# Pairs 0 and 1 of layer 0: residuals one pair later, pair 1's roots through TensorE, the second gate product ahead of the transposes

## The chip, the core and the metric

The kernel runs on one core of one Trainium2 chip. A core has TensorE (PE, matrix products into PSUM), VectorE (DVE), ScalarE (ACT), GpSimd (POOL), and SyncE (SP), whose queue issues the DMAs. Each engine works through its own queue in the order in which the program wrote it, and waits on semaphores for the others. The metric is the device time of one execution in microseconds; the median of three runs is compared.

## The reference

Two residual layers on one image `x` of 128 rows, 256 positions and 256 channels. Each layer first normalizes over 32 channel groups.

```
x = x + L0(_gn(x));   x = x + L1(_gn(x))        # _gn: 32 groups
L0:  m_norm = layer_norm(m);  z_norm = layer_norm(z)
     q, k, v = m_norm @ Wq.T, @ Wk.T, @ Wv.T    # 8 heads of 32
     b = z_norm @ Wb.T                          # bias per pair of positions and head
     gate = sigmoid(m @ Wg.T + bg)
     p = softmax(q k / sqrt(32) + b)            # 256 x 256 per row and head
     return (p v * gate) @ Wo.T + bo
L1:  4 heads of 64, softmax in a band of 16, projections w_in, w_out
```

Note that the gate is computed from `m` (the group-normalized rows), while Q, K and V are computed from `m_norm` (the same rows, layer-normalized over channels). Here `m` is `_gn(x)`, and the layer's result is added to `x`.

## The kernel before

**Stages.** A prologue loads `z` and `x`, takes the group statistics of `x` (tiles `M0` and `R0`, mean and reciprocal deviation per channel) and turns `z` into `eb`, the exponential of the bias for all heads. Layer 0 then walks over 64 pairs of rows; layer 1 follows. The change lies in the first three pairs of layer 0.

**One pair.** `class Pair` (L1244) holds the tiles of two rows of `x`. Its methods are steps:

- `centre` and `scale` (POOL) subtract `M0` and multiply by `R0`, giving `xg`. Each is one pass over 128x1024 values. `xg` has one buffer.
- `moments` (VectorE) takes the layer norm's statistics of `xg`, and `root` (POOL) raises the variances to the power -1/2, in place in one of two tiles `lrs`.
- `xgT`, the transposed group-normalized rows, is made in two ways. Pair 1 uses `turn`: eight TensorE transposes into two PSUM slots, and two ScalarE copies. From pair 2 on `blocks` loads 32x32 blocks of `x` by DMA, `turn_blocks` transposes them on VectorE and `scale_blocks` applies the group norm on ScalarE.
- `xnT`, the layer-normalized rows, is `xgT` times the roots, which must be spread over all partitions. `send` transposes the roots on VectorE and writes them to device memory with four DMAs; `fetch` reads them back into all partitions (`rs_r`); `normal` multiplies on POOL, in two halves. Pair 0, in the prologue, does it otherwise: `spread_roots` multiplies the roots, broadcast as weights, with the identity matrix on TensorE, and `normal_first` multiplies `xgT` by that PSUM tile on VectorE.
- `project` makes Q, K (from `xnT`) or the gate (from `xgT`), one half of the channels at a time: four matmul passes and one ScalarE eviction. `values` and `keep_values` make V.
- `scores(r, c)` makes the scores of row `r` and four heads and their exponentials; `add_bias` multiplies by `eb` on VectorE (`e`) and adds two key halves on POOL (`eboth`); `apply` makes the weighted values (`ov`) from `e` and the softmax sums (`su`) from `eboth` on TensorE; `gate` multiplies `ov` with the gate on VectorE.
- `invert` takes the reciprocals of the sums, and they go through device memory (`fetch_sums`); `normalize` applies them on POOL; `out_row` is the output product and `keep_row` adds `xt`.
- `residual` adds the output bias `bo` to `xt` on POOL, one pass over 128x1024 values. It must be done before the pair's first `keep_row`, and after `centre` has read `xt`.

**Order.** The loop over pairs, under `manual_schedule`, writes the order of every queue by hand. In turn `p`, `now` is pair `p`, `nxt` pair `p+1`, `nn` pair `p+2`, `was` pair `p-1` and `old` pair `p-2`; a name without a pair does nothing. The second half of a row's work is finished one pair later: `was.apply(1, es)` and `was.gate(1)` come in the next turn, `was.out_row(0)` at that turn's end and `old.out_row(1)` in the turn after. Turn 0 has a special order, since pair 1 isn't prepared in the same way as the later ones: `moments`, `root`, `send`, `fetch`, `turn`, `normal` for pair 1, and the residuals of pairs 1 and 0, stand inside it. The residual of a later pair stands at the end of the turn two before its own.

**Buffers.** Small products share two PSUM slots in turn (`mm`); a product waits until the slot's tile of two products ago has been read. Scores have two PSUM tiles, `eboth` two buffers for each half, `ov` and `su` one each.

Of the kernel before, what the change touches and what calls it, by code (L numbers as in the profile page):

```python
# [773 lines left out]
def fast_kernel(  # L774
# [215 lines left out]
    def mm(name):  # L990
        return ps_mm.tile([P, 512], F32, name=name, tag="mm")
# [544 lines left out]
    def some(n):  # L1536
        for _ in range(min(n, len(later))):
            later.pop(0)()
# [10 lines left out]
    def pair(p):  # L1549
        return Pair(p) if p < NP else Nobody()  # L1550
# [3 lines left out]
    def load_first():  # L1554

        by_block = x1[0][0:2].rearrange("s (i b) (k j a) -> k j b (s i) a", b=D0, k=KC, a=D0)
        for k in range(KC):
            for j in range(HQ):
                nc.sync.dma_start(
                    first[k][j * D0 : (j + 1) * D0].rearrange("b (i a) -> b i a", a=D0), by_block[k, j]  # L1560
                )
# [3 lines left out]
    now = nxt = nn = None  # L1565
# [131 lines left out]
    with tc.manual_schedule():  # L1697
        old = was = Nobody()
        es = nn3 = None
        for p in range(NP):  # L1700

            if p > 0:
                nxt.send()
            pss = now.scores(0, 0)
            if p == 0:
                now.values(0)
                now.keep_values(0)
                now.values(1)
            e0 = now.add_bias(0, 0, pss)
            was.apply(1, es)  # L1710
            if p == 0:
                now.keep_values(1)
                for r in range(2):
                    nxt.moments(r)
                nxt.root()
                nxt.send()
                now.project("gT", 0)
            pss = now.scores(0, 1)
            was.gate(1)
            nxt.fetch()  # L1720
            if p == 0:
                nxt.turn([mm("ps_x") for _ in range(KC)])
            es = e0, now.add_bias(0, 1, pss)
            if p == 0:
                nxt.normal()
            nn.centre()
            if p > 0:
                now.project("gT", 0)
                now.values(0)
                now.keep_values(0)  # L1730
            was.invert()
            was.fetch_sums()
            some(1 if p < NP - 2 else 3)
            nn.scale()
            now.project("gT", 1)
            if p > 0:
                nxt.turn_blocks()
            nn.blocks()
            if p == 0:
                nxt.residual()  # L1740
                now.residual()
            else:
                nxt.scale_blocks()
            if p < NP - 1:
                old.out_row(1)
                some(1 if p < NP - 2 else 3)
                old.keep_row(1)
                if p > 0:
                    now.values(1)
                    now.keep_values(1)  # L1750
            nn3 = pair(p + 3)
            if p > 0:
                nxt.normal()

            e0 = now.add_bias(1, 0, now.scores(1, 0))
            now.apply(0, es)
            pss = now.scores(1, 1)
            now.gate(0)
            es = e0, now.add_bias(1, 1, pss)
            was.normalize(0)  # L1760
            nn.moments(0)
            for m in range(KC):
                nxt.project("qT", m)
                nxt.project("kT", m)
            if p == NP - 1:
                load_first()
                old.out_row(1)
                old.keep_row(1)
                now.values(1)
                now.keep_values(1)  # L1770
                some(8)
            was.normalize(1)
            nn.moments(1)
            nn.root()
            nn.residual()
            some(3 if p < NP - 2 else 9)
            was.out_row(0)
            was.keep_row(0)
            old, was, now, nxt, nn = was, now, nxt, nn, nn3
        was.apply(1, es)  # L1780
        was.gate(1)
        was.invert()
        old.out_row(1)
        was.spread()
        old.keep_row(1)
        for r in range(2):
            was.normalize_last(r)
        for r in range(2):
            was.out_row(r)
            was.keep_row(r)  # L1790
        some(len(later))
# [29 lines left out]
    with tc.tile_pool(name="l1", bufs=2) as sb, tc.tile_pool(  # L1821
# [284 lines left out]
        def pair1(p):  # L2106
            return Pair1(p) if p < NP else Nobody()
# [36 lines left out]
        with tc.manual_schedule():  # L2144
            now, nxt = pair1(0), pair1(1)
# [18 lines left out]
            was = Nobody()  # L2164
            for p in range(NP - 1):
# [76 lines left out]
                was, now, nxt = now, nxt, nn  # L2242
# [44 lines left out]
@with_exitstack  # L2287
def mixer_kernel(ctx, tc, *args):

    nc = tc.nc  # L2290
    keep = ctx.enter_context(tc.tile_pool(name="verdict", bufs=1))
    verdict = keep.tile([1, 1], mybir.dt.int32, name="verdict")
    fast_kernel(tc, *args, verdict)
    again = nc.values_load(verdict[0:1, 0:1], min_val=0, max_val=1)
    with tc.If(again > 0):
        general_kernel(tc, *args)
# [53 lines left out]
```

## Time and profile before

| | |
|---|---|
| median of 3 runs | 3133.21 us (3131.51 to 3134.19) |
| the profiled execution's own time | 3134.36 us |
| its span, first to last instruction | 3132.6 us |
| mean granted TensorE clock | 0.985 |
| start of pair 0's first scores on TensorE | 215.93 us |
| start of pair 1's first scores | 242.27 us |
| start of pair 2's first scores | 277.68 us |
| start of pair 3's first scores | 305.11 us |

The profile is of one execution. The page gives each engine's busy time, its share in 40 slices of the span, the chain of work that ended last, and the costliest groups of instructions. The trace behind it can be cut to a stretch: the timeline lists an engine's instructions with the idle time before each and who ended it, and a table of stages gives the busy time of TensorE, its weight loads, VectorE, ScalarE and POOL, then the clock that TensorE was granted, the DMA engines' share and GB/s. The ends of matmuls are modelled: a group of matmuls that waits can be recorded as one long group without idle time. Instructions of one engine that follow each other overlap by a few hundredths of a microsecond in the records.

### The profile page before, as it was taken

How to read it: one execution, taken by the hardware profiler on the slowest of the kernel's cores; microseconds unless marked ns; L12 is line 12 of the kernel's file. 1: busy time of each engine (PE TensorE's matmuls, PEld its weight loads, DVE VectorE, ACT ScalarE, POOL GpSimd, SP SyncE). 2: the span in 40 equal slices, each digit the busy share in tenths (PEclk: the TensorE clock that was granted, in tenths of full speed). 3: DMA queues.
4: the chain of work that ended last, by engine and by line, in shares of the span. 5: the costliest groups of instructions: out<-in, count | busy, mean ns of one | idle time of the engine just before them, and what ended most of it. 6: DMA issues, size and time to landing. Idle time of an engine off the chain costs nothing.

```text
span 3132.6 us, 80584 instructions
## 1 busy us (share of the span) xinstructions
PE 3017.0 (96%) x33630; PEld 2096.3 (67%) x33630; DVE 2398.1 (77%) x4007; ACT 1574.6 (50%) x2639; POOL 2271.3 (73%) x1635
## 2 busy tenths in 40 slices
PE   5589999999999999999999999899999999999998
PEld 3345555655555565555555655588888888888886
DVE  7986777777777777777777777588888877777788
ACT  3454444444444444444444444355555555555554
POOL 3469998988899889889998987455555555555553
PEclk9799999999999999999999999899999999999999
DMA  9952333323333332333333232544343444343431
GB/s 360 389 173 59 97 71 99 93 66 91 99 99 69 99 97 65 89 98 99 69 99 99 64 92 71 117 93 94 92 95 92 95 92 94 90 97 88 98 93 53
DMA packets 690951, 328.16 MB, mean 105 GB/s; under 512 B 538673, under 2 KB 639921, under 8 KB 689425
## 3 DMA queue, kind: packets, MB, share of 16 engines
q1 hardware_dynamic: 686176, 320.28, 39.9%
q8 instruction: 266, 4.36, 0.6%
q10 hardware_dynamic: 4400, 2.63, 0.3%
q14 instruction: 109, 0.88, 0.1%
HBM read 254.09 MB, written 68.75 MB: 103 GB/s over the span
## 4 chain that ended last, share of the span: by engine, by line
PE 90%; DMA 4%; DVE 3%; issue 1%; POOL 1%; ACT 1%; SPq 0%; POOLq 0%; ACTq 0%; DVEq 0%
PE ps_p L1364 22%; PE ps_qk L1956 12%; PE ps_sc L1401 9%; PE ps_ov L1436 7%; PE ps_su_y L2088 7%; PE ps_v L1382 7%; PE ps_qk L1952 7%; PE ps_y L1491 7%; PE ps_o L2034 4%; PE ps_su L1444 3%; PE ps_sc L2009 3%; PE ps_su_y L2042 2%; DMA xa<-in_x_dram 1%; DVE st L1199 1%; DMA zt<-in_z_dram 1%
## 5 line engine op out<-in xcount | busy, mean ns | idle before, releaser
L1425 POOL TENSOR_TENSOR eboth<-e 128x512 f32<-128x512 f32 x512 | 746.9, 1479 | 175.9 <-PE ps_su L1444 95.5
L1421 DVE TENSOR_TENSOR e<-ps_sc,eb 128x1024 f32<-128x1024 f32 x384 | 458.2, 1221 | 290.5 <-ACT ps_sc L1413 289.9
L1413 ACT ACTIVATE ps_sc<-ps_sc 128x1024 f32<-128x1024 f32 x384 | 375.4, 1007 | 439.4 <-PE ps_sc L1401 308.0
L1401 PE MATMUL ps_sc<-qT,kT 32*128 32x256 f32 x4096 | 296.1, 401 | 0.1
L1919 POOL TENSOR_TENSOR dT<-xgT,dT 128x256 f32<-128x256 f32 x63 | 46.1, 731 | 315.7 <-ACT xgT L1905 315.7
L2020 POOL TENSOR_TENSOR e<-e,bw 128x384 f32<-128x384 f32 x256 | 248.4, 1001 | 10.7 <-ACT e L2018 10.7
L1401 PEld LDWEIGHTS ps_sc<-qT,kT 32*128 32x128 f32 x4096 | 186.3, 184 | 103.6 <-issue 90.6
L2088 PE MATMUL ps_su_y<-w_out,oT 128*128 128x256 f32 x1008 | 254.5, 385 | 0.9 <-DVE sums L2059 0.9
L1491 PEld LDWEIGHTS ps_y<-wo,oT 128*128 128x128 f32 x1024 | 194.7, 190 | 83.9 <-issue 44.7
L1364 PE MATMUL ps_p<-xgT,wg 128*128 128x512 f32 x512 | 249.1, 609 | 1.6 <-ACT xgT L1333 1.6
L1364 PE MATMUL ps_p<-xnT,wq 128*128 128x512 f32 x512 | 247.5, 605 | 1.5 <-POOL xnT L1351 1.4
L1436 PE MATMUL ps_ov<-e,v 128*32 128x256 f32 x4096 | 248.2, 383 | 0.0
L1491 PE MATMUL ps_y<-wo,oT 128*128 128x256 f32 x1024 | 243.1, 381 | 3.5 <-POOL oT L1481 2.7
L1382 PE MATMUL ps_v<-wv,xnT 128*128 128x256 f32 x1024 | 242.2, 379 | 0.0
L1364 PE MATMUL ps_p<-xnT,wk 128*128 128x512 f32 x512 | 240.7, 592 | 0.0
L1382 PEld LDWEIGHTS ps_v<-wv,xnT 128*128 128x128 f32 x1024 | 194.9, 190 | 54.7 <-issue 31.5
L2065 DVE RECIPROCAL rv<-sums 128x256 f32<-128x256 f32 x128 | 223.1, 1743 | 0.0
L1965 ACT ACTIVATE u<-ps_qk,bin_c 128x256 f32<-128x256 f32 x378 | 174.7, 477 | 94.9 <-PE ps_qk L1956 94.9
L2088 PEld LDWEIGHTS ps_su_y<-w_out,oT 128*128 128x128 f32 x1008 | 181.8, 190 | 22.4 <-DVE sums L2059 1.3
L1436 PEld LDWEIGHTS ps_ov<-e,v 128*32 128x32 f32 x4096 | 120.2, 110 | 109.2 <-issue 42.5
L1364 PEld LDWEIGHTS ps_p<-xnT,wk 128*128 128x128 f32 x512 | 97.2, 190 | 122.8 <-issue 122.8
L1371 ACT ACTIVATE gT<-ps_p,bg_c 128x512 f32<-128x512 f32 x128 | 88.0, 687 | 179.5 <-PE ps_p L1364 179.5
(229 smaller groups left out, 6553.3 us busy)
## 6 DMA issues: line engine op xcount, KB each, us to landing
xa<-in_x_dram SPq DMA_DIRECT2D x8, 4096.0 KB
xt<-in_x_dram SPq DMA_DIRECT2D x64, 512.0 KB
x<-xo SPq DMA_DIRECT2D x16, 2048.0 KB
xt<-x SPq DMA_DIRECT2D x64, 512.0 KB
rvb<-rsum SPq DMA_DIRECT2D x252, 128.0 KB
xs<-x SPq DMA_DIRECT2D x252, 128.0 KB
out_dram<-yo SPq DMA_DIRECT2D x63, 512.0 KB
xs<-in_x_dram SPq DMA_DIRECT2D x248, 128.0 KB
```

The costliest lines, as they stand in the source:

```text
L1364: nc.tensor.matmul(ps, w[:, k, m * P : (m + 1) * P], getattr(self, src)[:, k, :], start=(k == 0), stop=(k == KC - 1),)
L1382: nc.tensor.matmul(self.ps_v[:, b * C : (b + 1) * C], self.xnT[:, k, t * P : (t + 1) * P], wv[:, k, :], start=(k == 0), stop=(k == KC - 1),)
L1401: nc.tensor.matmul(self.pss[q // 2][:, q % 2, b, :], self.kT[rs, c, r * I + b * P : r * I + (b + 1) * P], self.qT[rs, c, r * I : (r + 1) * I],
L1413: nc.scalar.activation(self.pss[a], ps, AF.Exp)
L1421: nc.vector.tensor_tensor(es[a], pss[a], eb[:, h : h + 2], ALU.mult)
L1425: nc.gpsimd.tensor_tensor(t, es[a][:, :, 0, :], es[a][:, :, 1, :], ALU.add)
L1436: nc.tensor.matmul(ov[q * D0 : (q + 1) * D0, c, :], self.v[:, r, b, h * D0 : (h + 1) * D0], es[q // 2][:, q % 2, b, :], start=(b == 0), st ...
L1491: nc.tensor.matmul(self.ps_y[:, b * C : (b + 1) * C], self.oT[r][:, k, b * P : (b + 1) * P], wo[:, k, :], start=(k == 0), stop=(k == KC - 1),)
L1956: nc.tensor.matmul(to, lhs, rhs, start=start, stop=True, skip_group_check=True)
L2020: nc.gpsimd.tensor_tensor(e[:, q], e[:, q], bcast(bw.rearrange("p b w -> p (b w)"), 1, KC), ALU.mult)
L2065: nc.vector.reciprocal(self.rv[:, r, :], self.sums)
L2088: nc.tensor.matmul(self.y[:, b], self.oT[r][:, k, b * P : (b + 1) * P], w_out[:, k, :], start=(k == 0), stop=(k == KC - 1),)
```

## The change

Four things are moved or replaced, all in turns 0 to 2.

1. Roots of pair 1. `send`, `fetch` and `normal` of turn 0 go. In their place `spread_roots` stands after the products of `scores(1, 0)`, and `normal_first` after `add_bias(1, 0)`. This takes a VectorE transpose, five DMAs and two POOL passes out of turn 0, and puts in four TensorE products and two VectorE passes.
2. The second gate product of pair 0, `project("gT", 1)`, moves from after `nn.scale` to before `add_bias(0, 1)` and the transposes of pair 1. In TensorE's queue it now stands between the products of `scores(0, 1)` and the transposes, in ScalarE's its eviction stands before the two copies.
3. `add_bias(0, 1)` is written before `turn`. The order on each queue is not altered by this alone.
4. The residuals of pairs 1 and 0 leave turn 0. Pair 0's now stands in turn 1 and pair 1's in turn 2, after `nxt.normal` and before the `eboth` of `scores(1, 0)` in POOL's queue.

In SP's queue the loads of pair 2's blocks and of pair 3's rows now follow directly on the prologue's last loads. From turn 3 on all queues are as before.

```diff
                 for r in range(2):
                     nxt.moments(r)
                 nxt.root()
-                nxt.send()
                 now.project("gT", 0)
             pss = now.scores(0, 1)
             was.gate(1)
-            nxt.fetch()
+            if p > 0:
+                nxt.fetch()
+            else:
+                now.project("gT", 1)
+            es = e0, now.add_bias(0, 1, pss)
             if p == 0:
                 nxt.turn([mm("ps_x") for _ in range(KC)])
-            es = e0, now.add_bias(0, 1, pss)
-            if p == 0:
-                nxt.normal()
             nn.centre()
...
             nn.scale()
-            now.project("gT", 1)
             if p > 0:
+                now.project("gT", 1)
                 nxt.turn_blocks()
             nn.blocks()
-            if p == 0:
-                nxt.residual()
-                now.residual()
-            else:
+            if p > 0:
                 nxt.scale_blocks()
...
             if p > 0:
                 nxt.normal()
-
-            e0 = now.add_bias(1, 0, now.scores(1, 0))
+            if p in (1, 2):
+                was.residual()
+
+            pss = now.scores(1, 0)
+            if p == 0:
+                nxt.spread_roots()
+            e0 = now.add_bias(1, 0, pss)
+            if p == 0:
+                nxt.normal_first()
             now.apply(0, es)
```

## The prediction

> **What bounds the kernel now.** I read the page first: busy shares and slices, then the chain that ended last.
>
> ```profile
> PE 3017.0 (96%) x33630; PEld 2096.3 (67%) x33630; DVE 2398.1 (77%) x4007; ACT 1574.6 (50%) x2639; POOL 2271.3 (73%) x1635
> ...
> PE   5589999999999999999999999899999999999998
> ...
> PE 90%; DMA 4%; DVE 3%; issue 1%; POOL 1%; ACT 1%; SPq 0%; POOLq 0%; ACTq 0%; DVEq 0%
> ```
>
> TensorE is 90% of the chain. A microsecond that TensorE gains early in layer 0 is kept only if it is full from there on. So the second view is the chain cut to 150 to 420 us, around the pairs that the change touches.
>
> ```profile
> 240.71 4.69 POOL xt L1289 x2
> 245.40 4.88 POOL eboth L1425 x4
> 250.28 0.99 POOL lrs L1306
> 251.51 1.12 DVE e L1421
> 252.67 2.08 PE ps_sc L1401 x12
> 254.75 3.71 PE ps_p L1364 x4
> ```
>
> Here POOL, not TensorE, sets the end from 240.7 to 251.3: two residual adds, then pair 0's four `eboth` sums, then the roots of pair 2, whose transpose stands first in VectorE's queue. After 252.67 every long piece of this chain is PE. The third view is TensorE's timeline of the same place, with its idle time and who ended it.
>
> ```profile
> 226.10 1.98 PE L1364 MATMUL ps_p<-xgT,wg 128*128 128x512 f32 x4 [1.55 <-ACT xgT L1333]
> ...
> 234.83 2.36 PE L1364 MATMUL ps_p<-xnT,wq 128*128 128x512 f32 x4 [1.35 <-POOL xnT L1351]
> ...
> 246.67 0.63 PE L1444 MATMUL ps_su<-eboth,pick 128*32 128x256 f32 x4 [1.39 <-POOL eboth L1425]
> ```
>
> Three stalls: the second gate product waits for the copies of pair 1's transposes, Q of pair 1 waits for `xnT` behind the roots' trip through memory, and the sums of pair 0 wait for POOL. The fourth view, busy time by stages of 3.41 us, shows what the last one drags behind it: the clock column (after ACT and POOL) falls.
>
> ```profile
> 245.31:248.72 3.41, 1.25 (x8) 0.29 (x8) 0.00 (x0) 0.08 (x1) 3.41 (x4) 1.00 0.00 0
> 248.72:252.13 3.41, 2.86 (x12) 0.88 (x12) 0.83 (x2) 0.00 (x0) 3.41 (x4) 0.50 0.00 0
> 252.13:255.55 3.42, 3.31 (x15) 1.70 (x14) 3.42 (x4) 1.53 (x2) 3.42 (x2) 0.50 0.12 41
> 255.55:258.96 3.41, 3.41 (x6) 1.63 (x5) 1.98 (x2) 0.86 (x2) 3.41 (x4) 0.50 0.10 36
> ```
>
> [...] 0.50 for three such windows after one with 1.25 us busy; windows with 2.07 us busy (231.65 to 235.07) kept 1.00. [...] the `e<-e,eb` product at 252.53 took 2.13 us instead of 1.22 while POOL's residual ran to 253.58, and the next `eboth` 2.25 us instead of 1.26. [...] `rs_d` and `rs_r` took from 227.30 to 233.01.
>
> **The change part by part.** I carried each queue forward by hand from 219 us, in its written order, with the durations of the rows: 1.08 us for eight score products (two passes each), 1.75 for a whole gate, Q or K product, 1.75 for values, 1.77+0.98 for `apply`, 0.94 per exponential, 1.14 per `e` product, 0.62 per eviction, and on POOL 1.22 per `eboth` or `oT`, 2.31 per 128x1024 pass, 1.24 per `xnT` half, 0.98 per root. On the old order this lands at 263.9 for pair 1's `scores(1,0)` (trace 263.87), 276.1 for the output row (275.86) and 305.2 for the start of pair 3 (305.11), so the method is good to some 0.3 us here.
>
> Pair 0. The gate product moves ahead of the transposes: its slot was freed by the values' eviction at 223.1, so it runs 223.4 to 225.1 and the 1.55 us stall goes. ScalarE then has the gate's 0.69 us eviction before the copies, and the second transpose waits 0.3 us for that slot. VectorE no longer waits for POOL's roots (1.13 us) and transposes them (0.21); the `e` products start at 225.0 instead of 226.2. `scores(1,0)` ends at 228.2 with 0.6 us of waiting. Added: `spread_roots`, four products as eight passes, 1.15 us at 200.54 in the existing use for pair 0; it is on TensorE's path and costs all of it, 228.2 to 229.4 (roots ready 226.1, slot free 226.5). `normal_first` puts two VectorE passes of 0.68 us (row at 201.80) at 232.2 to 233.4; TensorE is in `scores(1,1)` until 233.2, so they hide, and delay only `gate(0)` and the last `e` products, whose cover is the 7 us of Q and K products. Q starts at 233.2 without a stall, and pair 1's scores at 240.2 instead of 242.3.
>
> POOL loses 2.5 us of `xnT`, its 3.58 us wait and 4.69 us of residuals: `centre` and `scale` of pair 2 run 228.7 to 234.5, the four sums 234.5 to 239.5, the roots end at 240.5. The sums of pair 0 are needed at 243.1, so that stall goes with 3.6 us of margin. The roots' transpose is done at 240.8, before the first exponentials of pair 1 (241.2), so VectorE's queue isn't held.
>
> SP loses four `rs_d` sends and one fetch. The four `xs` loads of pair 2 and the next `xt`, which had stood behind them until 228.97, are issued after the previous `xt` load, at 185.7. They go behind loads already queued that end by 193, and `xs` is needed only at 251. Cost taken: nothing; if they shared rather than queued, up to their own transfer time, some 8 us (DMA share 0.17 to 0.97 from 228 to 238), on the start-up chain.
>
> Sum to pair 1's `scores(1,0)`: 34.0 us of products lie between 215.93 and there. Before it took 47.9, so 13.9 were lost: 5.64 of idle in six gaps, about 3.1 for half clock from 252.67 to 258.96, the rest inside matmul groups whose records stretch while they wait. After: 34.0 + 1.15 + 0.9 of small waits = 36.1, at 252.1. Gain 11.8.
>
> **What the moved residuals take back.** In pair 1, between `normal` and `scores(1,0)`, POOL now does pair 0's residual, 2.31 us; queued behind it are four sums and `normalize(0)`, for which the output row waits. Chain: first sum 244.5, fourth ends 249.8, `centre`, `scale` to 254.5, `xnT` to 256.9, [...] residual 258.1 to 260.4, sums to 265.4, `normalize(0)` to 266.7. TensorE is there at 264.3 (in pair 1 there is no older output row, 1.75 us, to give POOL time): stall 2.4. In pair 2 the same insert, with the older output row there: POOL 294.9, TensorE 294.1, stall 0.9. From pair 3 on POOL's load is the old one; in the old trace it has 1.71 and 0.5 us of idle per pair, so nothing is handed on. Net: 11.8 - 2.4 - 0.9 = 8.4.
>
> The profiled execution took 3134.36 us (span 3132.6 and 1.8 around it); 8.4 less is 3126.0. The median of the runs is 1.15 lower, 3133.21, so 3124.8. I put it at 3125.0, a little above, for the next case.
>
> **The rivals.**
> 1. The clock falls in the new stall. A window with 2.4 us idle has 1.0 to 1.4 us busy if the stall lies inside it; 1.25 was enough before, 2.07 was not. [...] One dense window at half rate costs 1.7: 3126.5, at the edge of 0.2%. Against: the stall may straddle two windows.
> 2. POOL catches up and neither stall appears (its order leaves 3.3 us less than I think, [...]): 3133.2 - 11.8 = 3121.4. Against: `normalize(0)` of pair 1 in the old trace ended only 0.8 us before the output row.
> 3. Little gained: pair 0's sums stay late, or the early `xs` loads delay the start-up chain by most of 8 us: about 3130. For: TensorE's first transposes then still wait for POOL. Against: the 3.6 us of margin, and packets of the earlier `xt` that landed as queued.
> 4. Slower: the clock, once lowered at the stall of 264, stays at half [...]. Half clock for 17 us takes back the 8.4; for the 33 us to the start of pair 3 it costs 16.5, ending at 3141. Against: three windows at most were needed at 248.72, and in pair 2 TensorE is dense for 26 us.
>
> **How the numbers follow.** Within 0.2% of 3133.2 is 6.3 us, about what runs of this kernel can tell apart: faster means under 3126.9. Forecast 0.45, all but a few hundredths of it faster; rival 1 0.25, two thirds faster; rival 2 0.12, faster; rival 3 0.12, same; rival 4 and the like 0.06, mostly slower. Faster 0.73, same 0.22, slower 0.05. The range reaches from rival 2 with the runs' 1 us of scatter, 3120.5, to short of rival 3, 3129.5.
>
> **What would show it.** TensorE without idle before the second gate product, pair 1's Q and pair 0's sums; the clock at 1.00 from 245 to 260; `xnT` of pair 1 on VectorE; `scores(1,0)` of pair 1 near 252; a POOL-ended wait of about 2.4 us ahead of the first output row and of about 0.9 ahead of the next. I am wrong if a POOL wait repeats from pair 3 on, if the start-up chain before 215.9 has moved, or if half clock returns at 265.

## The result and the profile after

The changed kernel takes 3127.14 us (median of 20 runs, 3124.5 to 3129.91) against 3134.20 us for the kernel before (20 runs): 7.1 us less, a ratio of 0.9978 with a 95% interval of 0.9972 to 0.9984. The forecast was 3125.0 us, from a median of 3133.21. The profiled execution took 3127.13 us, its span is 3125.4 us.

The page of the changed kernel: busy shares, and the chain that ended last.

```profile
PE 3014.3 (96%) x33638; PEld 2097.3 (67%) x33638; DVE 2398.2 (77%) x4008; ACT 1575.7 (50%) x2639; POOL 2268.6 (73%) x1633
...
PE 92%; DMA 4%; DVE 2%; POOL 1%; ACT 1%; issue 0%; SPq 0%; ACTq 0%; POOLq 0%; DVEq 0%
```

Eight matmul records more are the four root products in two passes. TensorE's busy time is the same as before to 3 us, so most of the gain is idle time taken away. The 40 slices of 78 us are too coarse to show it: the place, 216 to 305 us, lies in the third and fourth, whose digits (8 and 9) are as before. TensorE's timeline of the changed kernel shows where (start, duration, instruction, and in brackets the idle time before it with its releaser; no bracket means none).

```profile
223.79 1.98 PE L1364 MATMUL ps_p<-xgT,wg 128*128 128x512 f32 x4
...
228.63 1.16 PE L1338 MATMUL ps_rs<-ident,lrs 128*128 128x128 f32 x8
...
233.52 1.98 PE L1364 MATMUL ps_p<-xnT,wq 128*128 128x512 f32 x4
...
243.41 1.05 PE L1444 MATMUL ps_su<-eboth,pick 128*32 128x256 f32 x16
...
252.54 1.15 PE L1401 MATMUL ps_sc<-qT,kT 32*128 32x256 f32 x16
...
267.26 2.63 PE L1491 MATMUL ps_y<-wo,oT 128*128 128x256 f32 x8 [2.17 <-POOL oT L1481]
269.82 2.09 PE L1401 MATMUL ps_sc<-qT,kT 32*128 32x256 f32 x16
...
297.43 1.99 PE L1491 MATMUL ps_y<-wo,oT 128*128 128x256 f32 x8 [0.96 <-POOL oT L1481]
```

The three old stalls (TensorE idle for 1.55 us at the gate product, 1.35 at Q, 1.39 and more at the sums) are gone, and two new ones stand ahead of the output rows of pairs 0 and 1, both ended by POOL. The chain of the changed kernel in that place:

```profile
256.50 1.18 POOL xnT L1351
257.67 1.04 issue
258.71 2.37 POOL xt L1289
261.30 0.97 issue
262.27 3.72 POOL eboth L1425 x3
265.98 1.23 POOL oT L1481
267.26 2.63 PE ps_y L1491 x8
```

`xt L1289` at 258.71 is pair 0's residual in its new place. (The two pieces "issue" of about 1 us belong, in POOL's own timeline, to the second `xnT` pass, 256.50 to 258.75, and to the first `eboth`, 261.04 to 262.30.) Both the output row at 267.26 (2.63 us, 1.89 when at speed) and the scores behind it (2.09 us instead of 1.15) are slow. The table of stages says why: busy time of TensorE, its weight loads, VectorE, ScalarE and POOL, then the granted clock, the DMA share and GB/s.

```profile
265.06:268.47 3.41, 1.24 (x7) 1.08 (x7) 0.00 (x0) 0.69 (x1) 3.41 (x4) 1.00 0.00 0
268.47:271.88 3.41, 3.41 (x24) 1.87 (x24) 0.81 (x2) 0.00 (x0) 3.26 (x2) 0.50 0.01 2
271.88:275.30 3.42, 3.42 (x64) 2.10 (x64) 2.31 (x3) 1.94 (x2) 0.92 (x1) 1.00 0.19 38
```

In the profiles of the kernel before and of the changed kernel the granted clock is recorded as 1.00 or 0.50 and changes 21 times each, and the changes lie whole multiples of 3.413 us apart, to 0.002 us. Below, the places of this grid are called edges and the stretches between them windows; where the clock did not change, an edge is an estimate, counted on in steps of 3.413 us from changes elsewhere in the same profile.

The new stall fell into one window (265.06 to 268.47) with 1.24 us busy, and the next ran at half clock. Before, half clock lasted three such windows from 248.72; these are gone.

A measure that leaves out the rest of the kernel is the stage from pair 0's first scores to pair 3's first scores in a profile. It is 89.1 us before (215.93 to 305.04) and 83.1 us after (216.27 to 299.35). I call it the front stage below. All its ends are read from TensorE's timeline; the 305.11 in the table of the kernel before comes from the chain, which shows that group of products 0.07 us later.

### The profile page after: what moved, and what is told of

It reads as the page before. It is cut to its first block, busy times and chain, and to the rows that moved or that the text cites. A ratio compares the mean times of both kernels' runs of the same rounds, so it can differ in the third digit from the quotient of the medians.

```text
span 3125.4 us, 80592 instructions
## 1 busy us (share of the span) xinstructions
PE 3014.3 (96%) x33638; PEld 2097.3 (67%) x33638; DVE 2398.2 (77%) x4008; ACT 1575.7 (50%) x2639; POOL 2268.6 (73%) x1633
## 3 DMA queue, kind: packets, MB, share of 16 engines
q10 hardware_dynamic: 4400, 2.63, 0.3%
## 4 chain that ended last, share of the span: by engine, by line
PE 92%; DMA 4%; DVE 2%; POOL 1%; ACT 1%; issue 0%; SPq 0%; ACTq 0%; POOLq 0%; DVEq 0%
PE ps_p L1364 21%; PE ps_qk L1960 13%; PE ps_sc L1401 9%; PE ps_ov L1436 8%; PE ps_su_y L2092 7%; PE ps_y L1491 7%; PE ps_qk L1956 7%; PE ps_v L1382 7%; PE ps_o L2038 4%; PE ps_su L1444 3%; PE ps_sc L2013 3%; PE ps_su_y L2046 2%; DMA zt<-in_z_dram 2%; DMA xa<-in_x_dram 1%; PE ps_t L1143 1%; DVE st L1199 1%
## 5 line engine op out<-in xcount | busy, mean ns | idle before, releaser
L1922 POOL TENSOR_TENSOR dT<-xgT 128x256 f32<-128x256 f32 x63 | 46.0, 730 | 183.2 <-ACT xgT L1909 183.2
```

## The experiments

All times given as "below" or "above" are differences of medians to the kernel before, run beside the version in question, with the ratio and its 95% interval. Two causes were to be told apart for what the change saved (POOL freed by the roots, theory A, or by the residuals, theory B), and three for what it cost (the place of the residuals, POOL's load as a whole, the clock).

**The changed kernel again.**

> The changed kernel itself, beside the others. Expected 7 us below the kernel before, as in its 20 runs; TensorE idle 2.2 us ahead of pair 0's output row and 1.0 us ahead of pair 1's.

Measured: 6.7 us below (ratio 0.9978, 0.9970 to 0.9986), front stage 83.1 us, half clock from 268.4.

**The residuals behind the first normalization.** The two passes stay in turns 1 and 2 and move only within POOL's queue.

```diff
             if p > 0:
                 nxt.normal()
-            if p in (1, 2):
-                was.residual()
...
             was.normalize(0)
+            if p in (1, 2):
+                was.residual()
             nn.moments(0)
```

> The residuals of pairs 0 and 1 stand in the same turns, but behind normalize(0) instead of ahead of the sums. Theory (the inserted residual makes the output row late and the idle time then halves the clock for a window): both stalls go, 2.2 + 1.0 us, and with them some 1.7 us of half clock; 11 to 12 us below the kernel before, near 3122.5. Rival (POOL's total load in these two turns is the limit, wherever the pass stands): a stall of about 2 us appears at the next pair's sums or scores instead, and the time stays within 1 us of the changed kernel's, 3127.

Measured: 9.8 us below (0.9968, 0.9956 to 0.9981), 3.1 us below the changed kernel run beside it, and less than the 11 to 12 expected. Front stage 78.0 us. Later, with the kernel that has the residuals in turn 0 beside it:

> The kernel with the residuals behind normalize(0) once more, beside the others. Stage from pair 0's first scores to pair 3's 78.0 us again, 9.5 to 11.5 us below the kernel before, and 2.5 us or more below the kernel with the residuals in turn 0.

Measured: 11.0 us below (0.9965, 0.9953 to 0.9977), 2.6 us below the kernel with the residuals in turn 0, front stage 78.0 us again. POOL's timeline of this second run:

```profile
263.72 1.26 POOL L1481 TENSOR_TENSOR oT<-oT,rvb 128x512 f32<-128x512 f32 x1
264.94 2.34 POOL L1289 TENSOR_TENSOR xt<-xt,bo_r 128x1024 f32<-128x1024 f32 x1
267.25 1.26 POOL L1481 TENSOR_TENSOR oT<-oT,rvb 128x512 f32<-128x512 f32 x1
```

and TensorE's:

```profile
265.03 1.99 PE L1491 MATMUL ps_y<-wo,oT 128*128 128x256 f32 x8
...
292.61 1.89 PE L1491 MATMUL ps_y<-wo,oT 128*128 128x256 f32 x8
```

The same pass, one place later, holds up the second row's normalization, which nothing waits for yet. No bracket stands before either output row, and the clock stays up. This version beats the changed kernel and the kernel before: its 12 runs have a median of 3123.1 us, against 3127.3 for the 27 runs of the changed kernel that stood beside the experiments.

**No residuals for pairs 0 and 1.** The two lines in turns 1 and 2 are deleted.

```diff
-            if p in (1, 2):
-                was.residual()
```

> Leaves out adding the output bias to the rows of pairs 0 and 1. Theory: what the two passes cost where they were put is all that the changed kernel lost, so 11 to 12 us below the kernel before, within 1 us of the kernel with the residuals behind normalize(0). Rival (POOL's total load): clearly faster than that kernel, by 2 us or more.

Measured: 8.6 us below (0.9974, 0.9963 to 0.9984), short of the 11 to 12 expected; front stage 77.9 us. That is 0.1 us shorter than with both passes present behind the normalization. POOL's load as a whole is thus not the limit in these turns; the place is. The whole time, 1.2 us above that kernel's, is not told apart from it (resampling the runs gives 0.6 us less to 3.1 us more).

**Work in the stall.** Two products whose result is not used go ahead of pair 0's output row.

```diff
+            if p == 1:
+                ps = mm("ps_fill")
+                for n in range(2):
+                    nc.tensor.matmul(ps, wg[:, 0, 0:P], now.xgT[:, 0, :], start=True, stop=True)
             was.out_row(0)
```

> The changed kernel with two products of 512 columns, 1.7 us, whose result is not used, in TensorE's queue ahead of pair 0's output row. Theory of the clock: the stall of 2.2 us stays (POOL ends it) but the window is no longer idle, so no half clock near 268 us, and the time is up to 1.7 us lower than the changed kernel's, as often as its clock falls there. Rival (the clock costs nothing, or falls for another reason): same time as the changed kernel, or the half clock still there.

The timeline of TensorE in this run:

```profile
265.97 1.88 PE L1784 MATMUL ps_fill<-xgT,wg 128*128 128x512 f32 x4
268.32 1.99 PE L1491 MATMUL ps_y<-wo,oT 128*128 128x256 f32 x8 [0.47 <-POOL oT L1481]
```

In the profile POOL still ends the wait, the clock stays at 1.00, and the front stage is 81.5 us, 1.6 less: what the theory asks for. The timed runs did not follow: 6.5 us below the kernel before, as the changed kernel. So both were run once more.

> The changed kernel with the two unused products ahead of pair 0's output row, once more. If the half clock near 268 us is frequent in the timed executions too, not only in the two profiled ones, the median lies 0.8 to 1.7 us below the changed kernel's of the same call; if it is rare there, the two medians agree within 0.5 us. Stage from pair 0's first scores to pair 3's: 81.5 us again, without half clock.

> The changed kernel for the comparison with the filled one: 6 to 8 us below the kernel before; stage 83.1 us if the clock falls ahead of pair 2, 81.4 if not.

Measured: 6.4 us below for the filled kernel (0.9980, 0.9973 to 0.9987), 6.0 for the changed one (0.9982, 0.9974 to 0.9990), medians 0.4 apart. The front stages are both 81.5 us: this third profile of the changed kernel kept its clock with the same stall of 2.17 us. So the clock falls in some executions and not in others (two profiles of three). The table of stages of this third profile, cut at its edges, shows what was different:

```profile
262.20:265.61 3.41, 2.67 (x7) 0.88 (x5) 1.10 (x5) 1.37 (x2) 3.41 (x3) 1.00 0.12 45
265.61:269.02 3.41, 1.99 (x12) 1.51 (x12) 0.00 (x0) 0.00 (x0) 3.41 (x4) 1.00 0.00 0
```

Here an edge, 265.61, lies inside the stall (264.86 to 267.03). In the two profiles where the clock fell, the stall lay inside one window, which was left with 1.24 and 1.25 us busy. The same stall of 2.16 us also stood across an edge, and the clock stayed, in the profiles of the kernels with the residuals alone (edge at 271.50, stall 270.15 to 272.31) and with the sends kept (edge at 270.04), below. Five profiles agree with this; an experiment that sets where the edge falls was not made.

It also weakens the filler's profiles: an edge fell into the place of the stall in both (267.66 and 266.12), so they do not show that the filler kept the clock. Over both rounds the filled kernel's 32 runs and the changed kernel's 27 differ by 0.1 us, with resampled medians from 0.8 lower to 0.9 higher. A mean cost of 1.6 us in the timed executions is excluded. A smaller one is not. An estimate: if the edges fall evenly, a stall of 2.17 us lies inside a window of 3.41 in 36% of the executions (1.24 of 3.41), and 1.6 us in these makes a mean of 0.6, too little for these runs to show.

**The roots alone.** The kernel before with the first change only.

```diff
                 nxt.root()
-                nxt.send()
                 now.project("gT", 0)
...
-            nxt.fetch()
+            if p > 0:
+                nxt.fetch()
...
-            if p == 0:
-                nxt.normal()
             nn.centre()
...
-            e0 = now.add_bias(1, 0, now.scores(1, 0))
+            pss = now.scores(1, 0)
+            if p == 0:
+                nxt.spread_roots()
+            e0 = now.add_bias(1, 0, pss)
+            if p == 0:
+                nxt.normal_first()
```

> The kernel before, with pair 1's roots spread by TensorE and its xnT made on VectorE, and nothing else changed: the residuals stay in turn 0, the second gate product stays behind the transposes. Theory A (POOL is freed mostly by the roots: 2.5 us of xnT and 3.6 us of waiting): pair 0's sums are no longer late by more than 0.5 us though both residuals still stand ahead of them, scores(0,1) of pair 1 wait some 2 us for VectorE, and the time is 7 to 8 us below the kernel before. Theory B (the residuals are what made the sums late): the sums stay 3 us or more late, and the gain is under 4 us.

TensorE's timeline of this kernel:

```profile
226.65 1.98 PE L1364 MATMUL ps_p<-xgT,wg 128*128 128x512 f32 x4 [1.55 <-ACT xgT L1333]
...
235.65 1.98 PE L1364 MATMUL ps_p<-xnT,wq 128*128 128x512 f32 x4 [1.05 <-DVE xnT L1346]
242.72 1.15 PE L1401 MATMUL ps_sc<-qT,kT 32*128 32x256 f32 x16
246.52 1.44 PE L1401 MATMUL ps_sc<-qT,kT 32*128 32x256 f32 x16
```

Measured: 7.0 us below (0.9977, 0.9968 to 0.9986), front stage 80.9 us. The second group of pair 1's scores starts 3.80 us after the first, so the sums between them are not late, with both residuals still ahead of them in POOL's queue. Theory A holds, and this one part gives as much as the whole change. The expected wait of 2 us at those scores was only 0.3 us (1.44 against 1.15), because TensorE came late itself: the 1.55 us stall at the gate product and 1.05 at Q are still there, and pair 1's first scores start 26.2 us after pair 0's. In the kernel with the gate product moved too and the residuals in turn 0, below, they start after 24.3 us, POOL's roots end at the same point (28.9 us after pair 0's start in both), and the wait is 2.1 us.

**The residuals alone.** The kernel before with the residuals moved as in the changed kernel.

```diff
-            if p == 0:
-                nxt.residual()
-                now.residual()
-            else:
+            if p > 0:
                 nxt.scale_blocks()
...
             if p > 0:
                 nxt.normal()
+            if p in (1, 2):
+                was.residual()
```

> The kernel before, with only the residuals of pairs 0 and 1 moved as in the changed kernel. Theory A: pair 0's sums come in time, but the stalls at the gate, at Q and at the next scores stay and the new ones ahead of the output rows (2.4 and 0.9 us) appear: 1 to 3 us below the kernel before. Theory B: 6 us or more below it.

TensorE's timeline:

```profile
235.56 2.77 PE L1364 MATMUL ps_p<-xnT,wq 128*128 128x512 f32 x4 [2.16 <-POOL xnT L1351]
...
272.31 1.99 PE L1491 MATMUL ps_y<-wo,oT 128*128 128x256 f32 x8 [2.16 <-POOL oT L1481]
...
300.91 1.99 PE L1491 MATMUL ps_y<-wo,oT 128*128 128x256 f32 x8 [0.97 <-POOL oT L1481]
```

Measured: 2.2 us below, not told apart from nothing (0.9995, 0.9986 to 1.0003), front stage 87.0 us. The same two stalls ahead of the output rows appear without the other parts of the change: they belong to the residuals. In this profile pair 1's first scores also start 28.8 us after pair 0's, 2.5 more than before: the roots came back from memory 0.8 us later, and a window of half clock followed, from 237.37. Why is open, so 87.0 does not price the moved passes exactly.

**The gate product alone.**

```diff
             if p == 0:
+                now.project("gT", 1)
                 nxt.turn([mm("ps_x") for _ in range(KC)])
...
             nn.scale()
-            now.project("gT", 1)
             if p > 0:
+                now.project("gT", 1)
```

> The kernel before, with only the second gate product moved ahead of the transposes. The 1.55 us stall goes, but Q of pair 1 still waits for the roots' trip through memory and ends at the same time: 0 us, within 0.5 us of the kernel before. Rival (each stall counts for itself): 1.5 us below it.

```profile
226.25 0.66 PE L1329 MATMUL ps_x<-ident,xg 128*128 128x128 f32 x4 [0.34 <-ACT gT L1371]
...
234.84 2.36 PE L1364 MATMUL ps_p<-xnT,wq 128*128 128x512 f32 x4 [1.34 <-POOL xnT L1351]
```

Measured: 0.1 us above (1.0001, 0.9993 to 1.0009). On this timeline of TensorE the stall of 1.55 us is gone and Q starts at 234.84 as before (234.83): it waits for POOL. The front stage is 88.3 us; the 0.8 less than before is half clock, which lasted two windows (250.49 to 257.32) and not three.

**The residuals back in turn 0.** The changed kernel without its residual part.

```diff
-            if p > 0:
+            if p == 0:
+                nxt.residual()
+                now.residual()
+            else:
                 nxt.scale_blocks()
...
-            if p in (1, 2):
-                was.residual()
```

> The changed kernel with its residuals put back into turn 0: roots and gate product as changed. Theory A (the residuals' move gives nothing net, since what it saves at the next scores it pays ahead of the output rows): from pair 0's first scores to pair 3's 80.5 to 81.5 us against 83.1 of the changed kernel and 89.1 of the kernel before; a wait of some 2 us before scores(0,1) of pair 1, none over 0.3 us ahead of the output rows; time as the changed kernel's or up to 2 us lower. Theory B (moving the residuals is needed for the gain): this stage at 85 us or more, and 3 us or more slower than the changed kernel.

```profile
247.20 1.13 PE L1401 MATMUL ps_sc<-qT,kT 32*128 32x256 f32 x12 [1.08 <-DVE e L1421]
255.35 1.15 PE L1401 MATMUL ps_sc<-qT,kT 32*128 32x256 f32 x16
```

Measured: 8.5 us below (0.9976, 0.9967 to 0.9985), front stage 80.8 us, against 81.5 (clock kept) and 83.1 (clock fallen) of the changed kernel. TensorE's timeline shows the price of the residuals in turn 0: `scores(1,0)` of pair 1 start 14.1 us after its first scores (241.24), 2.1 more than in the changed kernel (11.96). Between these scores and pair 0's output row Q of pair 2 waits 0.82 us for POOL's `xnT`, and the way there is 0.7 us longer than with the residuals behind the normalization. In all, measured against that kernel's front stage (78.0), the residuals cost 2.8 us in turn 0 and, with the clock kept, 3.4 in the place that the change gave them. Theory A holds.

**The sends kept.** The changed kernel with one line put back, so that SP's queue is held as before.

```diff
                 nxt.root()
+                nxt.send()
                 now.project("gT", 0)
```

> The changed kernel with the transpose and the four sends of pair 1's roots kept in turn 0 (nothing reads them), so that the loads of pair 2's blocks stand behind them in SP's queue again, near 228 us instead of 186. If the early loads delay the start-up, pair 0's first scores start at 215.9 as in the kernel before; if they don't, at 216.3 to 217.3 as in the other kernels without the sends. Stage to pair 3's first scores: within 0.5 us of the changed kernel's 83.1 (VectorE waits 1.1 us for POOL's roots before the e products); time within 1.5 us of it.

Measured: pair 0's scores start at 216.37, so the early loads of pair 2's blocks do not delay the start-up. The rest was a miss: 2.9 us below the kernel before (0.9991, 0.9982 to 0.9999), 3.1 to 4.2 us less than the changed kernel gained in its three comparisons, front stage 84.4 us. The roots' transpose waits 1.13 us for POOL in VectorE's queue again, the scores that wait for VectorE are late in two pieces, and the table of stages of this kernel shows a window of half clock in turn 0:

```profile
225.68:229.09 3.41, 2.12 (x17) 1.21 (x19) 2.45 (x3) 1.98 (x4) 1.98 (x3) 1.00 0.01 1
229.09:232.51 3.42, 3.42 (x19) 2.63 (x20) 1.31 (x2) 1.94 (x2) 3.42 (x3) 0.50 0.78 120
...
266.63:270.04 3.41, 1.46 (x4) 0.38 (x2) 0.00 (x0) 1.16 (x2) 3.41 (x3) 1.00 0.00 0
270.04:273.46 3.42, 3.21 (x28) 2.32 (x32) 0.81 (x2) 0.10 (x1) 3.42 (x4) 1.00 0.01 2
```

The last two lines are the stall ahead of pair 0's output row in this kernel (268.09 to 270.25, across the edge at 270.04): 1.46 us busy, and the clock stayed.

## Why the prediction was right, and where it missed

**The queues carried forward: right.** From pair 0's first scores to `scores(1,0)` of pair 1 the prediction had 36.2 us; measured 36.3 (216.27 to 252.54). The copy's wait was 0.34 us (0.3 expected), the roots' products took 228.63 to 229.71 (1.15 us), Q did not wait, the sums did not wait, and the clock stayed up from 245 to 260.

**The new stalls: right in place, mechanism and nearly in size.** 2.17 us expected as 2.4, and 0.96 expected as 0.9. The shift of the residuals behind the normalization, which removes both, shows the cause; a kernel without the passes is only 0.1 us shorter in the front stage.

**The clock: rival 1 happened in part.** It was given a chance of 0.25 and 1.7 us. It occurred in two profiles of three, with 1.6 us. The prediction's argument against it, that the stall may straddle two windows, is what the third profile shows. Two of the prediction's own three signs of being wrong came true: half clock returned near 265 (at 268.4), and pair 0 began later (216.27 for 215.93). The forecast held all the same, since the fall comes in some executions only. The prediction's limit for a fall was too simple: it leaned on windows with 2.07 us busy that kept their clock, and a window with 2.12 us lost it when the roots' sends were kept, while one with 1.46 us kept it.

**The term that was mis-sized.** Forecast 8.2 us below the median, measured 7.1. The front stage gave 6.0 us in the first profile of the changed kernel: 8.4 less the 1.6 of half clock, less 0.4 where Q of pair 2 took 2.37 us instead of 1.98 at 257.56, a wait that the sum did not have, and less 0.4 in waits too small to place. The time lost behind the Q wait was in the prediction, one pass too late: by its author's estimate 1.2 us passed between the end of `xnT` (256.9) and POOL's residual (258.1), while in the trace the second half of `xnT`, for which Q waits, took 2.26 us instead of 1.26 while VectorE's `e<-e,eb` product ran beside it (256.36 to 257.62). Outside the front stage the prediction assumed no change. There pair 0 began 0.34 us later, and 1.5 us of the two spans' difference of 7.2 lie behind pair 3's first scores: the kernel before had a window of half clock from 1969 us in its profile, the changed kernel had none there. Such windows come and go between profiles of one kernel (the one near 268 us in two profiles of the changed kernel, not in the third). In the third profile, with the clock kept, the front stage gave 7.6 us; less the 0.6 that the clock costs on average by the estimate above, that is 7.0, about what the medians of the changed kernel show (7.1, 6.7 and 6.0).

**Which part earns what: not asked sharply enough.** The prediction summed three parts and freed POOL of "2.5 us of `xnT`, its 3.58 us wait and 4.69 us of residuals" together. The first two were enough: the roots alone give 7.0 us. The parts do not add. The gate product alone gives nothing; with the roots it brings pair 1's first scores forward by 1.9 us, and the wait for POOL takes that back as long as the residuals stand in turn 0 (front stage 80.9 without it, 80.8 with it). The residuals alone give 2.2 us, not told apart from nothing; once the other two are changed, their move costs 0.7 us in the front stage with the clock kept (81.5 against 80.8). What the gate product is worth with the residuals behind the normalization was not measured.

**Rivals 2 to 4.** No stall vanished by itself (2); the start-up was not delayed by the early loads (3); the clock was back after one window, at 271.88 (4).

## What to carry to other kernels

When a pass is moved out of a crowded place in a queue, count what stands behind it in the new place and who waits for that: one place later, behind the item that the next engine needs first, the same pass was free here (front stage 78.0 us, 77.9 without it). Removing a stall is worth nothing while the next one on the same path waits for something else. Here the gate product gave nothing alone, and 1.9 us at pair 1's first scores once the roots no longer held Q back. The stalls of one chain should be removed singly on paper before their sum is believed.

## What the hardware showed that was not expected

- TensorE's recorded busy time in a window of 3.41 us did not alone decide whether the next ran at half clock. Windows with 1.24, 1.25, 1.62 (the gate product alone), 1.70 (the residuals alone) and 2.12 us (transposes and 32-row score products, with the sends kept) were followed by half clock; windows with 1.46 (the sends kept), 1.86 (the residuals alone) and 2.07 us (the kernel before) were not. A stall of 2.17 us was followed by half clock in the two profiles where it lay inside one window, and not in the three where an edge cut it.
- In the eleven profiles of kernels that send no roots in turn 0 or hold them unread, pair 0 starts at 216.1 to 217.3 us, and in the three with the old trip through memory at 215.9 to 216.0. In the first profile of the changed kernel POOL's work on `z` already shows it (212.90 for 212.57), before any changed instruction of TensorE, VectorE, ScalarE or POOL. The moved loads stand earlier, at 186, but with the sends kept they are at 228 again and pair 0 still starts at 216.37. It was not explained.
